# Another order for the gathers of the last read counts, and edge sums one attention step sooner, in a segmented attention kernel

## The chip, the cores and the metric

The kernel runs on one core of a Trainium2 chip. The core has five engines with queues of their own: TensorE (PE, matrix products), VectorE (DVE), ScalarE (ACT), GpSimd (POOL, which here issues all indirect gathers and scatters and does a few elementwise operations) and SyncE (SP, which issues the plain transfers). Sixteen DMA engines are shared by all queues. The metric is the device time of one execution in microseconds. All times in this document are microseconds unless marked otherwise.

## The reference, cut to what matters

```python
N, d = feat.shape                      # 16384, 256;  B = 8, LMAX = 3072
q = feat @ Wq; k = feat @ Wk; v = feat @ Wv          # 32, 32 and 256 columns
starts = jnp.searchsorted(bids, jnp.arange(B))
pos = jnp.arange(N) - starts[bids]
pad = lambda x: jnp.zeros((B, LMAX, x.shape[-1])).at[bids, pos].set(x)
mask = jnp.zeros((B, LMAX), bool).at[bids, pos].set(True)
scores = jnp.where(mask[:, None, :], jnp.einsum('bld,bmd->blm', pad(q), pad(k)), NEG)
rp = jnp.einsum('blm,bmd->bld', jax.nn.softmax(scores, -1), pad(v))
r = rp[bids, pos]
t = r @ Wt
tn = (t - t.mean(0)) / jnp.sqrt(t.var(0) + EPS) * gamma + beta
return feat + jax.nn.relu(tn)
```

The ids in `bids` are not sorted, so `pos` runs far outside a segment's table. A write outside the table is dropped, a negative position counts from the table's end, and of two tokens on one place the later wins. The read `rp[bids, pos]`, though, takes every token: a position outside the table reads the segment's first or last row. Three kinds of rows come out of this: rows that a token owns and that are read once or twice (their "read count"), the sixteen edge rows (first and last row of each segment), which are read by thousands of tokens, and rows of tokens that lost their place and read the winner's row. The mean and the variance over all tokens weigh every row by how often it is read.

## The kernel before

The owned rows of each of the eight segments are listed and gathered from `feat` in up to six tiles of 128 rows. In this data some segments fill four tiles, others more; products of unfilled tiles are skipped by a branch on TensorE. For each segment `e` there are six attention steps `u`, one for each tile of queries (`step`, which calls `attend` and `scale`): TensorE multiplies the exponentials with the values, VectorE takes the reciprocal of the denominators (`rdens`), and ScalarE (even `u`) or VectorE (odd `u`) scales the result into `tk`. After steps 3 and 5 SyncE stores the rows to `t_rows` in memory. Between the steps the next segment is made ready: transposes (`xt_main`, `xt_rest`), projections (`project`), values (`values`) and exponentials (`scores`). For the segment after that, `prefix`, `sizes` and `list_ahead` count the rows, and `list_part` makes the index list and issues the gathers.

The order is written out by hand. A small class records every operation on its engine's queue in the order in which the Python code runs, works out from the memory that it reads and writes which earlier operations it has to wait for, and sets semaphores accordingly. Each engine works through its queue in this order: an instruction that waits holds all behind it. A helper's line stands for all its operations (L803 for products, L878 for gathers, L831 for tensor-scalar operations), so the names of the tiles tell them apart. Short PSUM results are put into two banks in turn by `nb()`: each call takes the other bank, so a product waits until what was in that bank two calls before has been read. On TensorE a predicated (skipped) product's signal is given by the next product that isn't predicated.

Around the change, by line:

- `attend` (L1273) ends with the reciprocal (L1282). It then issues gathers that wait for this reciprocal: in segment 5 (`NB - 3`) one gather of read counts a step (`gather_reads`, L1197), for segment 6; in segment 6 (`NB - 2`) those of segment 7, and the three gathers of winners' rows (`gather_again`, L1201) from `t_rows` into `tl`.
- `rows()` (L1571) returns two lists. Parts of the first run from a work list by `slot()`; its part `e` issues the three gathers `ridl` from `row_of`. `slot(99)` after step 2 of segment 6 (L1815) runs what is left, the last row-wise sums `both` among it. The second list, `late`, is called by number: `late[0]` (`f`, L1606) multiplies the edge rows' numbers over the partitions on TensorE and makes the gather index `eidx` in eight VectorE instructions; `late[1]` (`h`, L1635) makes six one-hot tiles `sel` on GpSimd; `late[2]`, `late[3]` and `late[4]` follow in segment 7 with the weights.
- L1823 to L1825 call `late[0]` and `late[1]` after step 4 of segment 6.
- At the end of segment 6, GpSimd sets `none` to zero (L1856). In segment 7, after step 0, GpSimd gathers the edge rows of the first seven segments into `ecat` (L1751). The sequence of steps is 0, 1, 4, 5, 2, 3; after step 2, TensorE picks the edge rows of segment 7 with `sel`, and VectorE adds them to `ecat` (L1786), ahead of step 3's reciprocal.
- `moments` (L1337) adds rows and their squares, weighted by read counts, into `acc` on VectorE; `square` (L1307) is ScalarE's part. Rows of `tl` come first in segment 7 (L1760).
- After the loop, the products with `ecat` and `acc` (L1872, L1873) give mean and variance; then every group of output rows is put together, stored by SyncE, and the owned rows are scattered over them by GpSimd.
- At the head of a segment (L1790 to L1795) step 0 is followed by `prefix`, `sizes` and `list_ahead` for segment `e + 2`, then by scores, step 1 and `xt_rest`.

```python
            for t in ((), (), (), (0, 1), (2,), ())[u]:
                gather_again(t, paced)
            for t in ((), (0,), (1,), (), (2, 3), (4, 5))[u]:
                gather_reads(e + 1, t, paced)
```

Of the kernel before, what the change touches and what calls it, by code (L numbers as in the profile page):

```python
# [21 lines left out]
NB = 8  # L22
# [8 lines left out]
LT = 3  # L31
# [870 lines left out]
def fast_path(nc, feat, bids, wq, wk, wv, wt, gamma, beta, out, bad):  # L902
# [147 lines left out]
    def nb():  # L1050
        turn[0] += 1
        return ps_m[turn[0] % 2]
# [144 lines left out]
    def gather_reads(e, t, after):  # L1197
        m = e * FT + t
        pg.gather(reads_r[:, m : m + 1], reads_of, idx[:, m : m + 1], N, after=[after])
# [22 lines left out]
    def xt_rest(e):  # L1222
        b = nb()
        for h in range(DH):
            transposes(e, h, range(4, 6), b, h * QB)
        for h in range(DH):
            into_xT(h, QA, QA + QB, b[:, h * QB : (h + 1) * QB])

    def project(e, c, b=None):
        b = nb() if b is None else b  # L1230
        n = QA if c == 0 else QB
        for h in range(DH):
            pg.mm(
                b[:, 0:n], w4[:, h, :], xT[:, h, c * QA : c * QA + n],
                start=(h == 0), stop=(h == DH - 1), pred=over4(e, 4 * c),
            )
        if (e, c) == (0, 1):
            pg.mm(b[:, n : n + 1], ident[:], ones[:, 0:1])
        lo, n = c * QA, (QA if c == 0 else QB)
        qe, ke = q[e % 2], k[e % 2]  # L1240
        pg.act(qe[0:96, lo : lo + n], b[0:96, 0:n], AF.Identity, bias=cqk[0:96, :])
        pg.act(qe[96:P, lo : lo + n], b[0:32, 0:n], AF.Identity, bias=cqk[0:32, :])
        for t in range(n // P):
            g = 32 * t
            pg.copy("DVE", ke[g : g + 32, c, :], b[96:P, t * P : (t + 1) * P])
# [27 lines left out]
    def attend(e, u):  # L1273
        po = po_of[u] = nb() if e == NB - 1 and u in (2, 3) else ps_o[u % 2]
        src, w = (pa, u) if u < 4 else (pb, u - 4)
        for t in (0, 1, 2, 4, 5, 3):
            pg.mm(
                po[:, 0 : D + 1], src[:, t, w * P : (w + 1) * P], vs[e % 2][:, t, :],
                start=(t == 0), stop=(t == 3), pred=over4(e, max(t, u)),
            )  # L1280
        m = e * FT + u
        paced = pg.recip(rdens[:, m : m + 1], po[:, D : D + 1])  # L1282
        if e == NB - 3:
            gather_reads(e + 1, u, paced)
        if e == NB - 2:
            for t in ((), (), (), (0, 1), (2,), ())[u]:
                gather_again(t, paced)
            for t in ((), (0,), (1,), (), (2, 3), (4, 5))[u]:
                gather_reads(e + 1, t, paced)
        if u % 2 and e < NB - 1:  # L1290
            pg.ts(tk[:, m, :], po[:, 0:D], rdens[:, m : m + 1], ALU.mult)

# [390 lines left out]
    def step(e, u, more=None):  # L1683
        attend(e, u)
        if more is not None:
            more()
        scale(e, u)
        if (e, u) != (NB - 1, 1):
            lag.append((e, u))
# [36 lines left out]
    for e in range(NB):  # L1726
        last = e == NB - 1
        n = e + 1
        if e == 1:
            one, two, three_ = edges()  # L1730
            sides = [*side_count(0, below[:]), *side_count(1, above[:])]
            fills = fill_rows()
            work.extend([fills[0], *one, fills[1], two, *sides, fills[2], *three_, lambda: own_of(NB - 1)])
        if not last:
            size_of(n)
        pg.region_of((e,) if last else (e, n))
        if e == 0:
            xt_rest(0)
            values(0, 1)
            project(0, 1)  # L1740
            values(0, 2)
            scores(0, 0, range(4, 6))
            own_of(2)
            zero_fill(2)
        if last:
            for u in (0, 1, 4, 5, 2, 3):
                step(e, u)
                if u == 0:
                    scores(e, 1, range(4))
                    late[2]()  # L1750
                    pg.gather(ecat[:, 0, :], t_rows[0 : (NB - 1) * FW, :], eidx[:], (NB - 1) * FW)  # L1751
                    for g in range(FIRST, EARLY):
                        load_group(g)
                if u == 1:
                    scores(e, 1, range(4, 6))
                    late[4]()
                if u == 4:
                    late[3]()
                if u == 0:
                    lag[:0] = [(NB, t) for t in range(LT)]  # L1760
                if u == 5:
                    first = square(e, 1)
                    for g in range(EARLY, MID):
                        load_group(g)
                if u == 1:
                    pg.act(row_sum[:], ones[:], AF.Identity, scale=reads_r[:, e * FT + 1 : e * FT + 2])
                if u == 3:
                    any_ = hot[0 : 2 * NB, 0:2, :, :].rearrange("p k u x -> p (k u x)")
                    pg.mm(sums[:], none[0 : 2 * NB, :], any_, start=True, stop=False)
                    by_row(row_sum, first[0], first[2])  # L1770
                if u == 3:
                    while lag or squared:
                        if lag and len(squared) < 2:
                            squared.append(square(*lag.pop(0)))
                        else:
                            moments()
                else:
                    past(e)
                if u == 2:
                    b_e = ps_s[0]  # L1780
                    for u_ in (0, 4, 5, 1):
                        pg.mm(
                            b_e[:, 0:D], sel[:, u_, :], tk[:, e * FT + u_, :], start=(u_ == 0), stop=(u_ == 1),
                            pred=over4(e, u_),
                        )
                    pg.tt(ecat[:, 0, :], ecat[:, 0, :], b_e[:, 0:D], ALU.add)  # L1786
                    pg.act(ecat[:, 1, :], ecat[:, 0, :], AF.Square)
        else:
            busy = e + 2 < NB
            step(e, 0, lambda: (xt_main(n, 0), xt_main(n, 1)))  # L1790
            if e + 3 < NB:
                prefix(e + 2, e + 3)
                sizes(e + 2)
            if busy:
                list_ahead(e + 2)  # L1795
            scores(e, 1, range(4))
            past(e)
            slot()
            if e == NB - 2:
                load_group(0)  # L1800
            step(e, 1)
            xt_rest(n)
            project(n, 0)
            if busy:
                list_part(e + 2, 0)
            scores(e, 1, range(4, 6))
            past(e)
            slot(1 if busy else 2)
            step(e, 2, lambda: project(n, 1))
            if busy:  # L1810
                list_part(e + 2, 1)
            past(e)
            slot(1 if busy else 2)
            if e == NB - 2:
                slot(99)  # L1815
                load_group(1)
                load_group(2)
            if e + 3 < NB:
                zero_fill(e + 3)
            step(e, 3)  # L1820
            scores(n, 0, range(4))
            step(e, 4, lambda: values(n, 0))
            if e == NB - 2:  # L1823
                late[0]()
                late[1]()  # L1825
            past(e)
            if e + 4 < NB:
                own_of(e + 3)
            if not busy:
                slot(2)  # L1830
            if e == 3:
                losers()[0]()
            slot()
            step(e, 5)
            values(n, 1)
            past(e)
            if e == 3:
                losers()[1]()
            if e == NB - 4:
                prefix(NB - 1, NB)  # L1840
                sizes(NB - 1)
                pg.copy("DVE", armf[:], arm[:])
                pg.red(cnt_f[0:1, 0:1], armf[:])
                pg.ts(upto[:, NB + 1 : NB + 2], cnt_f[0:1, 0:1], 16.0, ALU.mult, 16.0 * (4 * NB + LT), ALU.add)
                todo, late = rows()
                work.extend(todo)
            scores(n, 0, range(4, 6))
            values(n, 2)
            past(e)
            slot()  # L1850
        if last:
            assert not lag and not squared
        pg.end_region()
        if e == NB - 2:
            slot(99)
            pg.set("POOL", none[:], 0.0)  # L1856
# [104 lines left out]
    for k in range(NG):  # L1961
# [24 lines left out]
        if 3 <= k < 3 + NB:  # L1986
            e = k - 3
# [96 lines left out]
```

## Time and profile before

| | |
|---|---|
| median of three runs | 328.13 (326.43 to 328.25) |
| profiled execution | 328.07 |
| its span, first to last instruction | 323.4 |
| mean granted TensorE clock | 0.874 |
| busy: PE, DVE, ACT, POOL | 252.1, 239.1, 151.0, 136.7 |
| bytes moved | 52.49 MB, mean 162 GB/s |

The stretches that matter here, in us from the span's start: segment 0 begins near 32, segment 6 runs from 193 to 212, segment 7 from 212 to 231, the statistics from 231 to 243, and the output from 243 to the end. How full each stretch is shows the page's second part (forty slices of 8.1 us, tenths of busy time, PEclk the granted clock in tenths, DMA the mean busy share of the sixteen DMA engines):

```profile
PE   5599699998998999899989999696666963632600
...
DVE  3845579989677686559577898963578999999930
...
POOL 7333307061080043304402572688030237887774
PEclk9999979999999999999999999978575798755555
DMA  3101104124055015301210124399596999998895
```

TensorE and VectorE share the load up to slice 27; then the DMA engines and VectorE, and at last GpSimd. One execution is profiled, so a duration in it has no spread of its own.

### The profile page before, as it was taken

The numbers are of one execution on the slowest core, as the hardware profiler recorded it, in microseconds if no ns is written. First come the engines' busy times: TensorE is split into PE (matmuls) and PEld (weight loads), VectorE is DVE, ScalarE is ACT, GpSimd is POOL, SyncE is SP. The second block draws the span as 40 slices with busy tenths as digits, with TensorE's granted clock in tenths as the row PEclk, the third lists the DMA queues.
The fourth block names the chain that finished last, engine by engine and source line by source line (L and its number), as shares of the span: only waits on it lengthen the run. The fifth ranks groups of instructions, "written<-read, shape, count | busy, mean of one in ns | idle before, by whom it ended". The sixth has DMA issues, their size and how long they took to land.

```text
span 323.4 us, 4634 instructions
## 1 busy us (share of the span) xinstructions
PE 252.1 (78%) x1279; PEld 165.0 (51%) x1279; DVE 239.1 (74%) x773; ACT 151.0 (47%) x294; POOL 136.7 (42%) x143
## 2 busy tenths in 40 slices
PE   5599699998998999899989999696666963632600
PEld 2465557665776678667866776474313321210200
DVE  3845579989677686559577898963578999999930
ACT  3136859874765574366547639774301221110000
POOL 7333307061080043304402572688030237887774
PEclk9999979999999999999999999978575798755555
DMA  3101104124055015301210124399596999998895
GB/s 103 32 25 31 36 2 132 47 66 128 3 102 152 0 49 125 101 4 47 76 34 1 51 90 156 144 346 388 181 372 255 375 402 393 421 396 343 313 377 193
DMA packets 21533, 52.49 MB, mean 162 GB/s; under 512 B 5488, under 2 KB 14786, under 8 KB 17530
## 3 DMA queue, kind: packets, MB, share of 16 engines
q1 hardware_dynamic: 15674, 41.37, 34.0%
q0 software_dynamic: 5280, 10.18, 10.8%
q10 hardware_dynamic: 544, 0.52, 0.5%
q8 instruction: 15, 0.25, 0.3%
q14 instruction: 20, 0.16, 0.2%
HBM read 26.27 MB, written 28.74 MB: 170 GB/s over the span
## 4 chain that ended last, share of the span: by engine, by line
PE 47%; DVE 24%; issue 9%; ACT 8%; POOL 7%; DMA 1%; POOLq 1%; DVEq 0%
PE ps L803 45%; DVE tk L822 6%; DVE f L822 5%; POOL out L894 4%; ACT pa L813 3%; PE ps L808 2%; ACT xT L813 2%; DVE junk L829 2%; ACT vs L818 2%; DVE k L819 1%; DMA ecat<-t_rows,eidx 1%; POOL sel L831 1%; DVE tk L1938 1%; DVE tk L1940 1%; POOLq L1072 1%
## 5 line engine op out<-in xcount | busy, mean ns | idle before, releaser
L878 POOL DMA_INDIRECT xs<-in_r_feat,idx x48 | 50.9, 1061 | 100.5 <-DVE idx L842 51.9
L803 PE MATMUL ps<-vs,pa 128*128 128x257 f32 x312 | 77.9, 395 | 4.1 <-ACT vs L818 3.8
L803 PEld LDWEIGHTS ps<-vs,pa 128*128 128x128 f32 x312 | 58.3, 194 | 17.4 <-ACT vs L818 5.9
L894 POOL DMA_INDIRECT out<-tk,idx x32 | 35.9, 1121 | 31.8 <-DVE tk L842 17.6
L803 PE MATMUL ps<-wvt,xT 128*128 128x256 f32 x156 | 38.0, 390 | 3.4 <-ACT vs L818 3.4
L803 PE MATMUL ps<-y,hot 32*128 32x256 bf16 x256 | 14.9, 366 | 28.5 <-DVE f L822 25.6
L818 ACT COPY f<-ps 128x1024 f32<-128x1024 f32 (+1 forms) x12 | 10.0, 834 | 57.7 <-PE ps L803 57.7
L803 PEld LDWEIGHTS ps<-wvt,xT 128*128 128x128 f32 x156 | 29.0, 191 | 13.5 <-ACT vs L818 4.6
L813 ACT ACTIVATE pa<-ps,mask 128x512 f32<-128x512 f32 x48 | 29.5, 686 | 12.1 <-PE ps L803 12.1
L803 PEld LDWEIGHTS ps<-y,hot 32*128 32x128 bf16 x256 | 6.8, 115 | 44.9 <-DVE f L822 36.5
L803 PE MATMUL ps<-f,ident 128*128 128x512 f32 x38 | 27.4, 845 | 1.3 <-DVE f L822 1.2
L822 DVE TENSOR_TENSOR f<-f,ps 128x1024 f32<-128x1024 f32 (+3 forms) x17 | 25.9, 1559 | 0.9 <-PE ps L803 0.9
L842 DVE SCALAR_TENSOR_TENSOR acc<-tk,reads_r,acc 128x256 f32<-128x256 f32 x45 | 21.5, 477 | 5.7 <-DMA reads_r<-reads_of,idx 4.2
L819 DVE COPY k<-ps 32x128 f32<-32x128 f32 x48 | 14.1, 294 | 15.6 <-PE ps L803 14.9
L813 ACT ACTIVATE xT<-ps,negx 128x512 f32<-128x512 f32 (+1 forms) x32 | 17.0, 582 | 17.3 <-PE ps L808 9.8
L818 ACT COPY vs<-ps 128x512 f32<-128x512 f32 x24 | 14.1, 589 | 20.9 <-PE ps L803 20.8
L813 ACT ACTIVATE q<-ps,cqk 96x512 f32<-96x512 f32 (+3 forms) x32 | 18.3, 573 | 10.4 <-PE ps L803 10.1
L855 DVE RECIPROCAL rdens<-ps 128x1 f32<-128x1 f32 x48 | 7.7, 160 | 19.6 <-PE ps L803 19.5
L803 PE MATMUL ps<-xT,w 128*128 128x512 f32 (+1 forms) x48 | 21.8, 581 | 0.0
L878 POOL DMA_INDIRECT reads_r<-reads_of,idx x12 | 13.2, 1098 | 19.9 <-DVE ge L831 11.7
L842 DVE SCALAR_TENSOR_TENSOR acc<-sq,reads_r,acc 128x256 f32<-128x256 f32 x45 | 21.5, 478 | 0.0
L813 ACT ACTIVATE pb<-ps,mask 128x256 f32<-128x256 f32 x48 | 19.2, 476 | 4.1 <-PE ps L803 3.8
(271 smaller groups left out, 433.0 us busy)
## 6 DMA issues: line engine op xcount, KB each, us to landing
f<-in_r_feat SPq DMA_DIRECT2D x16, 1024.0 KB, 8.1
out<-f SPq DMA_DIRECT2D x15, 1024.0 KB, 8.5
t_rows<-tk SPq DMA_DIRECT2D x8, 512.0 KB, 3.5
t_rows<-tk SPq DMA_DIRECT2D x8, 256.0 KB, 2.9
eb<-edge_of SPq DMA_DIRECT2D x16, 64.0 KB
out<-f SPq DMA_DIRECT2D x2, 512.0 KB, 2.7
xs<-in_r_feat,idx POOLq DMA_INDIRECT x48, 2.9
out<-tk,idx POOLq DMA_INDIRECT x39
```

What stands on the lines that cost most here:

```text
L803: "PE", lambda e: e.matmul(out, lhsT, rhs, start=start, stop=stop, skip_group_check=True),
L808: return self.op("PE", lambda e: e.transpose(out, in_, ident), [in_, ident], [out], pred=pred)
L813: "ACT", lambda e: e.activation(out, in_, func, bias=bias, scale=scale), [in_, *more], [out]
L818: return self.op("ACT", lambda e: e.copy(out, in_), [in_], [out])
L819: return self.op(eng, lambda e: e.tensor_copy(out, in_), [in_], [out])
L822: return self.op(eng, lambda e: e.tensor_tensor(out, a, b, op), [a, b], [out])
L829: lambda e: e.tensor_scalar(out, a, s1, s2, op0, op1, accum_out=accum)
L831: else e.tensor_scalar(out, a, s1, s2, op0, op1),
L842: else e.scalar_tensor_tensor(out, a, s, b, op0, op1),
L855: return self.op("DVE", lambda e: e.reciprocal(out, in_), [in_], [out])
L878: lambda e: e.indirect_dma_start(out=out, out_offset=None, in_=table, in_offset=bass.IndirectOffsetOnAxis(ap=ind, axis=0), bounds_check=n ...
L894: lambda e: e.indirect_dma_start(out=table, out_offset=bass.IndirectOffsetOnAxis(ap=ind, axis=0), in_=src, in_offset=None, bounds_check=n ...
```

## The change

Three orders change; no operation is added or removed.

1. In segment 6, `attend` issues the gathers of read counts for segment 7 two a step in steps 0 to 2, and all three gathers of winners' rows in step 3. Before, the read counts were spread over steps 1, 2, 4 and 5, and the winners' rows over steps 3 and 4.
2. `late[0]` and `late[1]`, the edge product with its index and the one-hot rows, are called before step 4 of segment 6 instead of after it. Since step 4 issues no gathers any more, and step 5 neither, all gathers of this segment stand ahead of the one-hots on GpSimd.
3. In segment 0 alone, `prefix`, `sizes` and `list_ahead` for segment 2 are called after step 1 and `xt_rest` instead of after step 0. The values passed to them are the same.

```diff
         if e == NB - 2:
-            for t in ((), (), (), (0, 1), (2,), ())[u]:
+            for t in range(2 * u, 2 * u + 2) if u < 3 else ():
+                gather_reads(e + 1, t, paced)
+            for t in range(LT) if u == 3 else ():
                 gather_again(t, paced)
-            for t in ((), (0,), (1,), (), (2, 3), (4, 5))[u]:
-                gather_reads(e + 1, t, paced)
...
             step(e, 0, lambda: (xt_main(n, 0), xt_main(n, 1)))
-            if e + 3 < NB:
+            if 0 < e < NB - 3:
                 prefix(e + 2, e + 3)
                 sizes(e + 2)
-            if busy:
+            if 0 < e and busy:
                 list_ahead(e + 2)
             scores(e, 1, range(4))
...
             step(e, 1)
             xt_rest(n)
+            if e == 0:
+                prefix(e + 2, e + 3)
+                sizes(e + 2)
+                list_ahead(e + 2)
             project(n, 0)
...
             scores(n, 0, range(4))
-            step(e, 4, lambda: values(n, 0))
             if e == NB - 2:
                 late[0]()
                 late[1]()
+            step(e, 4, lambda: values(n, 0))
             past(e)
```

On the queues this gives, for GpSimd in segment 6:

```
before: ridl x3, reads 0, reads 1, tl x3, reads 2, reads 3, sel x6, reads 4, reads 5, none, ecat
after:  reads 0, reads 1, ridl x3, reads 2, reads 3, reads 4, reads 5, tl x3, sel x6, none, ecat
```

On TensorE the edge product stands ahead of the values of segment 7 instead of behind their first pair, so the two banks of `nb()` swap their turns there; in segment 0 the two products of `prefix` stand behind step 1, with the same swap. SyncE's order doesn't change.

## The prediction

> **What bounds the kernel now.** I read the shares of the chain of waits first, then that chain in order of time between 186 and 242 us, then GpSimd's and VectorE's timelines there, because the change acts there. The chain over the whole span:
>
> ```profile
> PE 47%; DVE 24%; issue 9%; ACT 8%; POOL 7%; DMA 1%; POOLq 1%; DVEq 0%
> ```
>
> TensorE carries most of the span, so most of the span is out of this change's reach. But the seven per cent of POOL lie in one place, ahead of the statistics (start us, us, what):
>
> ```profile
> 217.12 0.71 POOL sel L831
> ...
> 217.93 1.91 POOL sel L831
> ...
> 224.80 4.58 DMA ecat<-t_rows,eidx
> ...
> 229.40 0.43 DVE ecat L822
> ...
> 229.85 0.42 ACT ecat L813
> 230.27 0.37 ACT tk L813
> ...
> 230.69 5.24 PE ps L803 x6
> ```
>
> The one-hot rows (sel) keep GpSimd busy, the gather of the edge rows (ecat) is issued after them, its landing releases VectorE's sum, and ScalarE's scaling and TensorE's last products follow. GpSimd's own timeline tells why that gather is so late; in brackets stand the idle time before an instruction and what ended it:
>
> ```profile
> 193.18 0.99 POOL L878 DMA_INDIRECT reads_r<-reads_of,idx  x1 [1.12 <-DVE tk L831]
> 199.50 0.99 POOL L878 DMA_INDIRECT ridl<-row_of,idxo  x1 [5.33 <-DVE tk L831]
> ...
> 203.47 1.75 POOL L878 DMA_INDIRECT reads_r<-reads_of,idx  x1 [0.30 <-issue]
> 206.56 1.25 POOL L878 DMA_INDIRECT reads_r<-reads_of,idx  x1 [1.35 <-DVE k L819]
> 208.51 0.99 POOL L878 DMA_INDIRECT tl<-t_rows,ridl  x1 [0.70 <-DVE zrow L842]
> ...
> 214.98 6.75 POOL L831 TENSOR_SCALAR sel<-edge,rcol 128x128 f32<-128x128 f32 x6
> 222.01 1.09 POOL L878 DMA_INDIRECT reads_r<-reads_of,idx  x1 [0.27 <-issue]
> 223.41 1.01 POOL L878 DMA_INDIRECT reads_r<-reads_of,idx  x1 [0.30 <-issue]
> 224.41 0.22 POOL L861 MEMSET none<- 128x128 bf16 x1
> 224.80 1.01 POOL L878 DMA_INDIRECT ecat<-t_rows,eidx  x1 [0.17 <-issue]
> ```
>
> From 208.51 on it never rests; before that it rests three times. VectorE behind it stands still twice:
>
> ```profile
> 226.80 0.48 DVE L842 SCALAR_TENSOR_TENSOR acc<-tk,reads_r,acc 128x256 f32<-128x256 f32 x1 [4.20 <-DMA reads_r<-reads_of,idx]
> ...
> 229.40 0.42 DVE L822 TENSOR_TENSOR ecat<-ecat,ps 128x256 f32<-128x256 f32 x1 [1.72 <-DMA ecat<-t_rows,eidx]
> ```
>
> Of these the second counts: without the first wait VectorE would merely reach the second sooner.
>
> [...] for the one-hots: they take from 0.71 to 1.91 us, and the longest lies at 217.93 under four 0.47 us accumulations of VectorE. [...] TensorE idled 2.39 us up to 39.12 and the granted clock was 0.50 from 41 to 43 us.
>
> **The change, part by part.**
>
> *1. GpSimd's order in segment 6.* The stretch from 199.50 to 224.80 us (25.30 us) holds twelve gathers (three ridl, six reads, three tl), six one-hots and a memset. The changed stream holds the same, all gathers first, so no work is removed: all that can be won is idle time and blocking.
> - Start. The first gather now waits for the reciprocal of step 0 (VectorE, 197.66 to 197.82). From such a release to the gather it took 0.76, 0.83 and 0.85 us (206.56, 199.50, 208.51), so it starts at 198.6 instead of 199.50: 0.9 us won.
> - Rests. The two reads of step 0, the three ridl and the two reads of step 1 run back to back at a pitch of 1.30 us to about 207.5; the release of step 2 (205.80) and of step 3 (207.66) are past by then. The rests of 1.35 and 0.70 shrink to the 0.30 of plain issue: 1.05 + 0.40 = 1.45 us.
> - Blocking. Two reads took 1.75 and 1.25 instead of 1.0 beside VectorE's work; another gather may meet it now. Won 0 to 1.0; I take 0.25.
> - One-hots. Six take 6.75 us; at the shortest, 0.71 each, it would be 4.3. Part 2 brings four accumulations (215.26 to 216.96) forward, out of their time. Won 0 to 2.4; I take 0.5.
>
> Sum 0.9 + 1.45 + 0.25 + 0.5 = 3.1 us: the ecat gather at 221.7 instead of 224.80. Its landing took 4.58. The DMA queue is fuller there (409 to 434 GB/s between 220 and 223 against 272 to 401 from 224 to 227): a reads gather issued at 222.01 released VectorE at 226.80, 4.8 us; the tl gathers took 5.6 to 6.9, the ridl ones 2.3. I take 4.7, losing 0.1, with bounds of 2.3 either way.
>
> *What is queued behind.* The tl gathers go from 208.51, 209.81 and 211.15 to about 210.3, 211.6 and 213.0, and with 6.4 us of landing are there at 216.7, 218.0 and 219.4. ScalarE squares them at 217.04 (two) and 219.01, ahead of the scaling of steps 1 and 4 of the last segment in its queue; it loses about 1 us. VectorE's sums of these rows follow. Both must be done at about 226.4, when the gather lands, and before they had idled 1.2 (ScalarE at 221.78) and 1.12 + 4.20 us there, the latter two on reads that have now landed long ago: no cost. Without that cover each us of lateness would cost one.
>
> *2. Edge sums one step sooner (late[0] and late[1] ahead of step 4).* One product of 0.39 us now stands before the values of the next segment and waits for VectorE's reduction ending at 205.60: TensorE, free at 204.6, loses 1.0 us. In return the two PSUM banks swap turns: the second pair of values, which waited 2.72 us for ScalarE's copy until 209.59, now waits for VectorE's last read of the edge product, 208.8. VectorE's chain of eight small instructions moves ahead of one reciprocal; ScalarE's scaling waits 0.2 us longer, beside its own backlog. [...] at 0.50 eight products of the last segment took 3.12 instead of 1.98 us. TensorE may so come 0.7 to 2.2 us sooner into the last segment. I count that at nothing by itself: the cover is the ecat gather, for which TensorE idles from 228.2 to 230.7 anyhow. One remainder: the six last products ran 5.24 us at clock 0.50; if the clock falls later they gain 0 to 1.0. I take 0.25.
>
> *3. Segment 0: prefix, sizes and list_ahead of segment 2 after xt_rest.* Thirteen VectorE instructions and two tiny products move behind step 1. The product waited for a PSUM bank and held attention behind it:
>
> ```profile
> 39.12 0.18 PE L803 MATMUL ps<-lm,tri 128*128 128x1 bf16 x1 [2.39 <-ACT xT L813]
> ...
> 42.13 2.65 PE L803 MATMUL ps<-xT,w 128*128 128x512 f32 x4
> ```
>
> Attention step 1 now starts at 36.8. But the banks swap here too: the projection (42.13) now needs the bank that ScalarE's next pair of xT copies reads, and these stand behind four exponentials (to 41.69) and take 0.84: 42.55. There TensorE has idled 2.6 us; at full clock the projection takes 1.88 (as at 60.28), at the halved one 2.65. VectorE, idle for 1.76 us until 44.83, waits for its end at 44.45 to 45.2, then runs without a rest to 58. So −0.35 to +0.9 us, passed on whole; I take 0.3 lost. The moved VectorE work fits into its idle time.
>
> *4. Behind the statistics.* From 243.49 VectorE, and from 265.89 GpSimd (a put every 1.29 us up to 318.81), work without a rest longer than 1.1 us; the DMA engines are full from 251 on, but with transfers that start after the statistics. So what is won at 229.40 is won at the end.
>
> Sum: 3.1 − 0.1 + 0.25 − 0.3 = 2.95 us. The profiled execution took 328.07 (span 323.4 and 4.67 around it), 0.06 under the median of the three runs: 328.07 − 2.95 = **325.1 us**.
>
> **The rivals.** One per cent is 3.28 us, about what a measurement of this kernel can tell from no change; the line lies at 324.85.
> - *The larger gain.* The one-hots run nearly free (4.8 us, 2.0 won instead of 0.5) and the gather lands in 3.9. For it: five 1 MB loads that now crowd the queue from 206 to 222 may go sooner with part 2. Against: VectorE's sums still have to be made. 325.1 − 1.5 − 0.8 = 322.8.
> - *It doesn't do what it says.* GpSimd's work ahead of the gather is unchanged; blocking and one-hots win nothing, the gather lands in 5.5, segment 0 loses 0.9: 328.07 − 2.35 + 0.9 + 0.9 = 327.5.
> - *Slower: the tl rows become the wait.* Behind three 1 MB loads (about 7.9 us at 400 GB/s) plus two more and their stores they could land far later. From the third row's landing L it is a square, two sums, two reciprocals and two more pairs of sums to the edge sum, about 2.8 us, so it decides from L = 223.6 and is slower than before from 226.6, 13.6 us after issue. At L = 230 it gives 328.07 + 3.4 + 0.3 = 331.8. Against: no gather here took over 7.6.
>
> **The numbers.** Forecast 0.72 (own range 323.6 to 326.6), larger gain 0.13, nothing done 0.10, slower 0.05. The forecast's 0.72 falls about half on each side of 324.85. Faster 0.36 + 0.13 = 0.49; within one per cent 0.36 + 0.10 = 0.46; slower 0.05. Range 322.8 to 327.6: it takes in the two middle rivals' times; the bounds of single terms don't add up in one run.
>
> **What would show it.** Step 1: the first reads gather near 198.6, no rest of GpSimd over 0.4 us up to the one-hots, which start at 214 to 215; ecat follows them at once near 221.7 and VectorE's wait on reads (4.20) is gone. Step 2: no 2.72 us wait of TensorE at 209.6. Step 3: attention at 36.8, VectorE's key copies between 44.5 and 45.3. Wrong, if VectorE waits for tl rows or squares when ecat has landed, if the gather lands over 6 us after issue, or if segment 1 starts over 1 us later.

## The result and the profile after

Before, the median was 328.13 (326.43 to 328.25); after, 323.9 (323.04 to 325.25). The ratio of the runs is 0.9887 with an interval of 0.9837 to 0.9936: 1.1% faster, 3.7 us, with 2.1 and 5.3 as the interval's ends. The profiled execution after took 323.04, its span is 318.4. A ratio compares only the runs within 1.5% of the fastest of their kernel (further down 2 of 4 for parts 1 and 2 at first, 3 of 5 with the ecat gather ahead of the one-hots, 4 of 20 with the tl gathers late, 11 of 23 for before beside the single parts), so the medians of all runs are given with it.

Executions of one kernel differ: 27 runs of before on one chip lay between 321.87 and 329.32. Much of that arises ahead of segment 0, as the second row of the table shows (the kernel before, profiled again). So stages are compared from the first reciprocal of segment 6 on. Times are those at which VectorE, GpSimd or TensorE starts the work named, read from the timelines; "again" is a second profile of the same kernel, and the last four rows are experiments further down.

| kernel | first attention product | key copies, segment 1 | first reciprocal, segment 6 | ecat gather issued | ecat sum | last products done | first output sum | last put |
|---|---|---|---|---|---|---|---|---|
| before | 33.88 | 44.83 | 197.66 | 224.80 | 229.40 | 235.96 | 243.49 | 318.81 |
| before, again | 30.00 | 39.26 | 192.08 | 219.57 | 223.66 | 230.21 | 237.82 | 313.13 |
| after | 32.68 | 44.27 | 197.27 | 219.79 | 226.66 | 231.91 | 239.15 | 313.10 |
| after, again | 34.21 | 44.51 | 197.33 | 219.60 | 225.75 | 231.03 | 238.27 | 312.22 |
| part 1 alone | 33.90 | 44.85 | 197.84 | 220.27 | 227.03 | 231.16 | 238.49 | 313.77 |
| parts 1 and 2 | 34.16 | 45.12 | 198.11 | 220.35 | 227.19 | 233.65 | 241.29 | 316.56 |
| parts 1 and 2, again | 33.06 | 44.00 | 196.81 | 219.55 | 225.38 | 229.51 | 236.88 | 310.84 |
| the same, third load held | 32.98 | 43.92 | 196.75 | 219.87 | 222.90 | 228.00 | 235.38 | 313.19 |

From the first reciprocal of segment 6 to the last put it is 121.15 and 121.05 before, 115.83 and 114.89 after: 5.2 to 6.3 us less. Both profiles of before agree to 0.1 us here, while their ends lie 5.7 us apart, which is why this stretch carries the argument. It has a spread too, though: the two profiles of parts 1 and 2 take 118.45 and 114.03. Of these 4.4 us, 2.3 lie in the last products, 1.6 behind them and 1.0 in the gather's landing, with 0.5 the other way in its issue. What is steady is the issue of the ecat gather: 27.1 and 27.5 us after the first reciprocal of segment 6 in the two profiles of before, 22.2 to 23.1 in the six below them, all of kernels with part 1.

The chain of waits over the span, after:

```profile
PE 41%; DVE 26%; ACT 11%; issue 9%; POOL 6%; DMA 4%; another core or an unknown queue 1%; POOLq 1%; DVEq 0%; SPq 0%
```

and the same chain in order of time at the end of segment 7 (start us, us, what):

```profile
219.42 0.20 POOL none L861
...
219.79 6.85 DMA ecat<-t_rows,eidx
226.64 0.02 issue
226.66 0.43 DVE ecat L822
...
227.12 0.42 ACT ecat L813
227.54 0.37 ACT tk L813
227.91 0.04 issue
227.95 3.94 PE ps L803 x6
```

The path still runs over the ecat gather. It is issued 5.0 us sooner (4.6 counted from the first reciprocal of segment 6), but its landing takes 6.9 us instead of 4.6, and the six products take 3.9 instead of 5.2. GpSimd's timeline after (in brackets the idle time before an instruction and what ended it):

```profile
198.19 0.99 POOL L878 DMA_INDIRECT reads_r<-reads_of,idx  x1 [4.40 <-DVE rdens L855]
...
203.39 1.47 POOL L878 DMA_INDIRECT ridl<-row_of,idxo  x1 [0.30 <-issue]
205.17 1.00 POOL L878 DMA_INDIRECT reads_r<-reads_of,idx  x1 [0.30 <-issue]
...
212.98 1.00 POOL L878 DMA_INDIRECT tl<-t_rows,ridl  x1 [0.31 <-issue]
214.08 5.29 POOL L831 TENSOR_SCALAR sel<-edge,rcol 128x128 f32<-128x128 f32 x6
219.42 0.20 POOL L861 MEMSET none<- 128x128 bf16 x1
219.79 1.09 POOL L878 DMA_INDIRECT ecat<-t_rows,eidx  x1 [0.16 <-issue]
```

No rest is over 0.31 us, and the one-hots take 5.29 instead of 6.75. VectorE's timeline after:

```profile
215.72 0.17 DVE L855 RECIPROCAL rdens<-ps 128x1 f32<-128x1 f32 x1 [3.55 <-PE ps L803]
...
226.66 0.42 DVE L822 TENSOR_TENSOR ecat<-ecat,ps 128x256 f32<-128x256 f32 x1 [1.95 <-DMA ecat<-t_rows,eidx]
```

Its wait for read counts has gone; the one for ecat has stayed, 1.95 instead of 1.72. The wait at the head of segment 7 is 3.55 us instead of 2.44 (at 215.04 before). ScalarE's timeline shows where it comes from ("remote" is a release that the profile can't name):

```profile
213.90 0.58 ACT L818 COPY vs<-ps 128x512 f32<-128x512 f32 x1 [3.88 <-remote]
```

This copy reads TensorE's second values of segment 7, and TensorE had gone on to the attention behind them at 210.35.

### The profile page after: what moved, and what is told of

Read it like the earlier page. It is cut to its first block, busy times and chain, and to the rows that moved or that the text cites. A ratio compares the mean times of both kernels' runs of the same rounds, so it can differ in the third digit from the quotient of the medians.

```text
span 318.4 us, 4632 instructions
## 1 busy us (share of the span) xinstructions
PE 249.3 (78%) x1279; PEld 162.2 (51%) x1279; DVE 238.8 (75%) x773; ACT 150.3 (47%) x294; POOL 133.8 (42%) x143
## 4 chain that ended last, share of the span: by engine, by line
PE 41%; DVE 26%; ACT 11%; issue 9%; POOL 6%; DMA 4%; another core or an unknown queue 1%; POOLq 1%; DVEq 0%; SPq 0%
PE ps L803 39%; DVE tk L822 6%; DVE f L822 5%; POOL out L894 4%; ACT pa L813 4%; ACT xT L813 2%; PE ps L808 2%; DMA ecat<-t_rows,eidx 2%; ACT vs L818 2%; DMA t_rows<-tk 2%; DVE junk L829 2%; DVE k L819 1%; DVE tk L1942 1%; DVE tk L1944 1%; ACT xs L818 1%
## 5 line engine op out<-in xcount | busy, mean ns | idle before, releaser
L894 POOL DMA_INDIRECT out<-tk,idx x32 | 34.4, 1075 | 28.4 <-DVE tk L842 19.2
L803 PE MATMUL ps<-f,ident 128*128 128x512 f32 x38 | 29.0, 893 | 1.7 <-DVE f L822 1.2
L813 ACT ACTIVATE q<-ps,cqk 96x512 f32<-96x512 f32 (+3 forms) x32 | 18.4, 573 | 13.6 <-PE ps L803 13.2
L878 POOL DMA_INDIRECT reads_r<-reads_of,idx x12 | 12.0, 1003 | 23.0 <-DVE ge L831 11.7
```

The source lines that it names most:

```text
L803: "PE", lambda e: e.matmul(out, lhsT, rhs, start=start, stop=stop, skip_group_check=True),
L813: "ACT", lambda e: e.activation(out, in_, func, bias=bias, scale=scale), [in_, *more], [out]
L878: lambda e: e.indirect_dma_start(out=out, out_offset=None, in_=table, in_offset=bass.IndirectOffsetOnAxis(ap=ind, axis=0), bounds_check=n ...
L894: lambda e: e.indirect_dma_start(out=table, out_offset=bass.IndirectOffsetOnAxis(ap=ind, axis=0), in_=src, in_offset=None, bounds_check=n ...
```

## The experiments

### The three parts, one by one

Part 1, the gathers' order, is the first hunk of the diff alone:

```diff
-            for t in ((), (), (), (0, 1), (2,), ())[u]:
+            for t in range(2 * u, 2 * u + 2) if u < 3 else ():
+                gather_reads(e + 1, t, paced)
+            for t in range(LT) if u == 3 else ():
                 gather_again(t, paced)
-            for t in ((), (0,), (1,), (), (2, 3), (4, 5))[u]:
-                gather_reads(e + 1, t, paced)
```

> Part 1 of the change alone: two read-count gathers a step in steps 0 to 2 and the three tl gathers in step 3 of segment 6, on the kernel before; the edge product stays behind step 4 and segment 0 as it was. GpSimd's order is then already that of the changed kernel. Theory A (filled rests of GpSimd bring the gain): GpSimd without a rest from about 198.6 us on, ecat gather issued at 220 to 222 instead of 224.80, time 323.5 to 325.5. Rival B (the product and the swap of PSUM banks in part 2 bring it): within 0.5 us of before, 327.6 to 328.6. Rival C (the order in segment 0 brings it): the same as B. Also looked at: TensorE's 2.72 us wait at 209.6 should stay, since the banks don't swap.

Measured: 323.07, just below theory A's range, ratio 0.9837 (0.9790 to 0.9884). The ecat gather went out at 220.27 and its sum came at 227.03, 29.19 after the first reciprocal of segment 6 instead of 31.74. Part 1 alone gains as much as the whole change: its ratio is no worse than the whole change's 0.9887, and its last put comes 115.93 after that reciprocal, against 115.83 and 114.89. That parts 2 and 3 add anything to it is not shown.

Part 2, the edge product one step sooner, is the last hunk alone (`late[0]` and `late[1]` ahead of step 4).

> Part 2 alone: late[0] and late[1] before step 4, gathers of segment 6 in the old steps, so that GpSimd makes the one-hots between the second and the third tl gather and issues tl 2 and reads 2 to 5 behind them. Theory A: GpSimd's rests at 199.5 and 206.6 stay and the ecat gather is issued at 224 to 225 as before; third tl row and the reads land after 221, and VectorE waits for them; 327 to 329.5. Rival B: TensorE's shorter wait at 209.6 gives 324 to 326 by itself.

Measured: 325.74 (320.7 to 326.42), in rival B's range, but too uneven for a ratio; before had 327.95 beside it. SyncE's timeline has the three loads of segment 7:

```profile
211.75 1.97 SPq L1722 DMA_DIRECT2D f<-in_r_feat  x3
```

and VectorE's the ecat sum, without a wait ahead of it:

```profile
228.02 0.41 DVE L822 TENSOR_TENSOR ecat<-ecat,ps 128x256 f32<-128x256 f32 x1
```

The loads start at 211.75 instead of 213.12, as TensorE gets there sooner. The gather goes out at 223.91, only 0.9 us sooner than before, yet VectorE doesn't wait for it: it landed within 4.1 us, and the sum is 30.16 after the first reciprocal, 1.6 better. In this profile, then, part 2 is worth something without part 1; the times do not settle it.

Part 3, segment 0, is the middle hunks alone.

> Part 3 alone: prefix, sizes and list_ahead of segment 2 after step 1 and xt_rest in segment 0. Theory A: no gain, from attention step 0 to the first key copy 11.3 to 11.9 us instead of 11.0, and 328.0 to 329.0 in all. Rival C: 324 to 326.

Measured: 328.5, ratio 1.0048 (1.0018 to 1.0078). The medians of all runs, 328.5 and 327.95, lie only 0.55 us apart, so the loss of 1.6 us that the ratio gives is not shown. In the profile, segment 0 loses nothing: from the first attention product to the key copies it takes 10.39 instead of 10.95. VectorE waits longer for the ecat gather, issued at 223.45:

```profile
230.12 0.42 DVE L822 TENSOR_TENSOR ecat<-ecat,ps 128x256 f32<-128x256 f32 x1 [3.88 <-DMA ecat<-t_rows,eidx]
```

It landed after 6.65 us. SyncE's timeline tells more. It has a fourth load in this segment, which stands ahead of the gather here:

```profile
222.37 0.33 SPq L1722 DMA_DIRECT2D f<-in_r_feat  x1
```

That is 1.1 us ahead of the gather. Part 2 alone issues this load behind its gather (227.58). What that means for the landing is taken up where the prediction is discussed.

Parts 1 and 2 together, without part 3:

> Parts 1 and 2, without part 3 (segment 0 as before). Theory A: as the changed kernel or up to 0.9 us faster, 323.0 to 324.5, since part 3 was priced at 0.3 us lost (-0.35 to +0.9). Rival C (segment 0 brings the gain): 326 to 328. From attention step 0 of segment 0 to the first key copy of list_part (11.0 us before, 11.6 in the changed kernel's profile) it should be 11.0 again.

Measured: 322.73 (317.26 to 326.1), ratio 0.9740 (0.9652 to 0.9829), four uneven runs; it is repeated below. Its profile, of the execution of 326.1, is the row "parts 1 and 2" of the table.

### What the landing of the ecat gather depends on

All three loads of segment 7 held until the gather has landed, in the changed kernel (the first waits, the others are behind it on SyncE):

```diff
-                    pg.gather(ecat[:, 0, :], t_rows[0 : (NB - 1) * FW, :], eidx[:], (NB - 1) * FW)
+                    edges_in = pg.gather(ecat[:, 0, :], t_rows[0 : (NB - 1) * FW, :], eidx[:], (NB - 1) * FW)
...
-                        load_group(g)
+                        load_group(g, [edges_in] if g == FIRST else ())
```

> After with one wait added: the first of the three loads of feat that SyncE issues in segment 7 (at 215.47 in after) waits until the ecat gather has landed, and the two loads and the stores behind it on SyncE with it. Theory A, the gather's 6.87 us of landing are queueing behind these loads: with the load of segment 6 long drained, the gather lands 2.3 to 4.0 us after its issue, near 222.5 to 224, VectorE's ecat sum comes before the last reciprocal has to wait for it, and the end of segment 7 is bound by its own attention instead: last products at 226 to 227.5. The loads are late by 7 to 8 us, which may hold the output at 244 to 250; time 321 to 325. Theory B, the gather's landing is a fixed latency plus its own descriptors: it still takes 6 to 7 us, the loads are later for nothing, time 324 to 328. ScalarE's 3.9 us stall at 210 to 213.9 comes before these loads: unchanged under both.

Measured: 327.08, beside 328.37 for before, ratio 0.9982 (0.9952 to 1.0012). GpSimd's timeline has the gather's issue:

```profile
220.55 1.10 POOL L878 DMA_INDIRECT ecat<-t_rows,eidx  x1 [0.16 <-issue]
```

and SyncE's the loads that wait for its landing:

```profile
223.50 1.43 SPq L1722 DMA_DIRECT2D f<-in_r_feat  x3
```

The loads were released at 223.50, so the gather had landed in 2.95 us: theory A on the landing, though not on the time, which it put at 321 to 325. The sum came 29.2 us after the first reciprocal of segment 6, hardly sooner than in the changed kernel (29.4): VectorE no longer waits for the gather, but TensorE's attention of segment 7 is late here (first reciprocal at 218.42). And the loads are paid for: from the first output sum to the last put it took 79.20 us, against 73.95 and 75.32 after and before.

The gather moved ahead of the one-hots, behind step 5 of segment 6:

```diff
             step(e, 5)
+            if e == NB - 2:
+                pg.gather(ecat[:, 0, :], t_rows[0 : (NB - 1) * FW, :], eidx[:], (NB - 1) * FW)
+                late[1]()
             values(n, 1)
```

> After with the ecat gather moved from segment 7 to the end of segment 6, ahead of the one-hot rows, and the one-hots with it. Theory A, the chain gather order - one-hots - ecat landing is what still sets the end: the gather is issued when the last store of rows has landed, near 215, at most 217, lands by 222, the wait of VectorE for it (1.95 us in after) is gone, and the last six products start 1 to 2 us sooner, near 226 to 227; the time is 1 to 2.5 us less than after's 323.9, 321.5 to 323. Theory B, segment 7's attention, late by ScalarE's stall, sets the end just as well: the wait for the gather goes but the sum becomes late for the one-hots' product, ScalarE or step 3; time within 0.7 us of after. The one-hots, now behind the gather on GpSimd, end near 221 to 223; over 225 they would be the new wait, and the time then over 325.

Measured: 326.86, beside 328.37 for before; ratio 0.9883 (0.9825 to 0.9941). GpSimd's timeline:

```profile
220.17 1.00 POOL L878 DMA_INDIRECT ecat<-t_rows,eidx  x1 [3.85 <-DMA t_rows<-tk]
221.26 7.15 POOL L831 TENSOR_SCALAR sel<-edge,rcol 128x128 f32<-128x128 f32 x6
```

It waits for the store of segment 6's rows, 3 us past the latest time expected, and the one-hots, now behind it, end at 228.4, late enough to be the new wait that the expectation names. VectorE's wait for the gather is gone, yet its sum comes 29.1 us after the first reciprocal of segment 6, hardly sooner than in the changed kernel (29.4): theory B in that.

The two loads of segment 6 moved to segment 7, so that none is in flight from 205 to 212:

```diff
-                load_group(1)
-                load_group(2)
...
-                    for g in range(FIRST, EARLY):
+                    for g in range(1, EARLY):
```

> After with the two loads of feat of segment 6 (issued at 205.43) moved to segment 7, in front of the other three: no load is in flight between 205 and 213. Theory A, ScalarE's stall (3.88 us in front of its copy at 213.90, released by nothing that it waits for) [...]: the copy runs within 1 us of the end of TensorE's values, near 210.5 to 211.5, VectorE's first reciprocal of segment 7 comes at 212 to 213.5 instead of 215.72. Theory B, the stall comes from GpSimd's gathers being denser: it stays at 3 to 5 us. The price under both: five loads after 212 crowd the queue until about 226, so the ecat gather lands later (7 to 9 us), and the time is between 322 and 327.

Measured: 324.55, beside 328.37 for before; ratio 0.9892 (0.9860 to 0.9925). ScalarE's timeline:

```profile
215.83 0.58 ACT L818 COPY vs<-ps 128x512 f32<-128x512 f32 x1 [4.52 <-remote]
```

The stall stays without the loads of segment 6, so theory A falls for these; the five loads begin at 212.15, 0.8 us into the wait. The gather, now behind five loads, was in 7.6 us after its issue.

### Controls, and a mechanism of the slower rival

In parts 1 and 2, the tl gathers behind the one-hots:

```diff
-            for t in range(LT) if u == 3 else ():
-                gather_again(t, paced)
+            if u == 3:
+                paced_of["tl"] = paced
...
                 late[1]()
+                for t in range(LT):
+                    gather_again(t, paced_of["tl"])
```

> Parts 1 and 2 of the change without part 3, and the three gathers of winners' rows (tl) issued behind the one-hot rows instead of ahead of them: GpSimd issues no gather between the last read counts (about 209 to 210) and the one-hots' end (about 216), the tl gathers run at 216 to 220 and the ecat gather after them near 220.5. Two questions. The late rows: the prediction's slower rival put 2.8 us from the landing of the third tl row to the edge sum, deciding from a landing at 223.6. With 5.6 to 6.9 us of landing the third row is there at 225 to 226.5, so VectorE's ecat sum should come at 228 to 229.3 instead of 227.2, 1 to 2 us of loss: 324 to 326 where parts 1 and 2 had a median of 322.7. If the rows don't matter, time as parts 1 and 2. The stall: theory A, TensorE's signal for the second values of segment 7 (and with it ScalarE's copy) is late because GpSimd issues gathers back to back just then: with the one-hots there instead, the copy runs at 211 to 212 with under 1 us of wait. Theory B, it has to do with something else that the change moves: the wait of 4 to 5 us stays.

> The changed kernel itself, beside parts 1 and 2 alone on the same chip, to see what part 3 is worth in their company. From part 3 alone (ratio 1.0048, 1.6 us) theory A says 1 to 2 us slower than parts 1 and 2 alone. Theory B, part 3 costs only its 0.3 to 0.6 us in segment 0 and the rest of 1.6 us was the ecat gather's landing behind other loads: within 0.7 us of parts 1 and 2. Its ratio to before should again be near 0.9887; its profile should again show ScalarE's copy of the second values waiting 3 to 5 us for TensorE's signal near 214, if that belongs to the order and not to one execution.

> Parts 1 and 2 without part 3 once more, with five rounds: as the version that may beat the changed kernel. Theory A: 321.5 to 323, a ratio to before of 0.980 to 0.985. Theory B: the lone run of 317.3 of the first look was an outlier of that chip and it stands where after stands, 0.986 to 0.989.

> The kernel before, profiled in the same way as the experiments, as a control for three waits read from one execution each. If ScalarE's late copy belongs to GpSimd's new order, its second copy of values near 212 waits under 1 us here, as in the first profile of before, while the smaller late signals of TensorE near 75 and 94 us, which part 2 and part 3 alone show too, may appear. The ecat gather should again be issued at 224 to 225, and land 4.6 to 6.7 us later, depending on whether the fourth load of segment 7 (222.85) is in front of it.

Measured on one chip: the tl gathers late, 326.32 and ratio 0.9918 (0.9865 to 0.9972); the changed kernel, 321.56 and 0.9899 (0.9826 to 0.9972); parts 1 and 2, 320.74 and 0.9867 (0.9799 to 0.9934), a ratio that is theory B's; before, 326.54. The profiled execution of before took 322.61; its ecat gather landed in 4.1 us, less than expected, and its second copy of values waited 1.99 us (1.91 in the first profile). The intervals of the second and third ratio overlap, so what part 3 costs in company is not settled. ScalarE's timeline with the tl gathers late:

```profile
222.27 0.42 ACT L813 ACTIVATE sq<-tl 128x256 f32<-128x256 f32 x1 [6.36 <-DMA tl<-t_rows,ridl]
```

and TensorE's:

```profile
224.48 2.07 PE L803 MATMUL ps<-tk,sel 128*128 128x256 f32 x4 [7.24 <-ACT pb L813]
```

The first tl row landed at 222.25, instead of 215.6 in parts 1 and 2. ScalarE stands before its square, the scaling and exponentials behind it wait, and TensorE with them for 7.24 us. The third row came at 224.2, and the edge sum at 227.53: 3.3 us behind, where the rival had put 2.8. In time, the ratios put the loss against parts 1 and 2 at 0.0051, 1.7 us, with overlapping intervals; by the medians of all runs it is 5.6 us, nearly the whole gain, and in the profiles the stretch to the last put is 120.30 instead of 114.03. The wait is shown, its size is not settled.

The second profile of the changed kernel, ScalarE's timeline:

```profile
210.62 0.59 ACT L818 COPY vs<-ps 128x512 f32<-128x512 f32 x1 [0.53 <-PE ps L803]
```

and VectorE's:

```profile
216.79 0.50 DVE L842 SCALAR_TENSOR_TENSOR acc<-tl,ones,acc 128x256 f32<-128x256 f32 x1 [1.79 <-DMA tl<-t_rows,ridl]
...
225.75 0.42 DVE L822 TENSOR_TENSOR ecat<-ecat,ps 128x256 f32<-128x256 f32 x1 [2.64 <-DMA ecat<-t_rows,eidx]
```

The 3.88 us stall is not there: the same kernel has it in one execution and not in another, so the order alone does not bring it. It cost little, too: the reciprocal at the head of segment 7 is 3.3 us sooner without it (212.43), the ecat sum 0.9. And in the kernel before itself the one-hots took 7.11 us in the second profile, 6.75 in the first:

```profile
209.40 7.11 POOL L831 TENSOR_SCALAR sel<-edge,rcol 128x128 f32<-128x128 f32 x6
```

### A version that may beat both

Parts 1 and 2, and only the third load held: as in the first diff of the part before, with `g == EARLY - 1` in place of `g == FIRST`.

> Parts 1 and 2 without part 3, and only the third of the three loads of feat in segment 7 held until the ecat gather has landed. In the look at parts 1 and 2 the gather went out at 219.55 and landed at 225.35, 5.8 us, with three loads of 1 MB queued from 211.7 on; with all three held it landed 2.9 us after its issue, but the output took some 4 us more. Theory A, the gather lands when what was queued ahead of it has gone, and one load of 1 MB is 2.6 us at the 400 GB/s seen there: it lands 2.5 to 4 us after issue, near 222.5 to 223.5, VectorE's 3.0 us wait for it goes, the last products start 1.5 to 2.5 us sooner; and one late load of three is made up for, as the output is bound by GpSimd's puts: ratio 0.980 to 0.984, median 318.5 to 320. Theory B, the late load is given back in the output as with three: ratio 0.985 to 0.990, the wait gone all the same. Theory C, the load held isn't what the gather queues behind: it still takes over 5 us.

Measured: 321.11, ratio 0.9836 (0.9801 to 0.9871). The windows view (stretch, length; busy time and instructions of PE, PEld, DVE, ACT and POOL; granted clock, DMA share, GB/s) of parts 1 and 2:

```profile
220.00:222.00 2.00, 2.00 (x6) 1.63 (x5) 2.00 (x8) 1.97 (x7) 0.65 (x1) 0.50 1.00 418
222.00:224.00 2.00, 2.00 (x7) 1.12 (x6) 0.36 (x1) 0.99 (x3) 0.00 (x0) 0.67 1.05 363
```

and with the third load held:

```profile
220.00:222.00 2.00, 2.00 (x6) 1.55 (x5) 2.00 (x8) 1.97 (x7) 1.18 (x1) 0.50 0.21 64
222.00:224.00 2.00, 2.00 (x7) 1.24 (x6) 1.15 (x4) 1.57 (x5) 0.00 (x0) 0.71 0.12 39
```

With two loads ahead the queue is nearly empty from 220 on (64 and 39 GB/s instead of 418 and 363), and the gather lands in 3.0 us instead of 5.8. The ecat sum is 2.5 us sooner, the first output sum 1.5, and then 3.9 us are lost to the last put (77.81 against 73.96): theory B's mechanism, though the ratio lies in theory A's range. The likely reason is the 3.3 us in which the DMA engines idled (2 us at a share of 0.21, 2 us at 0.12). That the output can hardly make them up is an estimate: in the changed kernel the share was 0.95 to 1.02 from 255 to 290, and 0.75 to 0.78 from there to 300. The chain with the third load held shows what would be next:

```profile
211.16 6.68 DMA tl<-t_rows,ridl
217.84 0.02 issue
217.87 0.42 ACT sq L813
218.28 0.36 ACT tk L813
218.65 0.37 ACT pb L813
219.02 0.04 issue
219.07 8.91 PE ps L803 x25
```

VectorE's wait for ecat is down to 0.52 us and off the chain: a tl row releases ScalarE's square, and that holds TensorE. It is faster than before; whether it beats parts 1 and 2 or the changed kernel the overlapping intervals do not tell (0.9836 against 0.9867 and 0.9899).

## Why the prediction was right

The forecast, 325.1, was 1.2 us above the measured median, and the larger gain's 322.8 was 1.1 below it. The mechanism was the right one: GpSimd's order brings the ecat gather forward, and the end with it. But four terms were off and partly cancelled, so the closeness of the sum is in part luck. From the first reciprocal of segment 6 to the last put, first profile of each kernel:

| term | forecast, won | measured, won | from |
|---|---|---|---|
| ecat gather issued | 3.1 | 4.62 | 27.14 and 22.52 after the reciprocal |
| its landing | −0.1 | −2.27 | issue to sum, 4.60 and 6.87 |
| last products | 0.25 | 1.31 | sum to products done, 6.56 and 5.25 |
| behind | 0 | 1.66 | products done to last put, 82.85 and 81.19 |
| sum | 3.25 | 5.32 | |

The first two terms, which are the forecast's mechanism, won 2.35 instead of 3.0. The last two won 2.97 instead of 0.25. That is luck as far as the runs show: each of them varies by about as much between two profiles of one kernel, as shown below.

*Where the path lies.* The seven per cent of POOL do not lie in one place. The page lists the chain by line:

```profile
PE ps L803 45%; DVE tk L822 6%; DVE f L822 5%; POOL out L894 4%; ACT pa L813 3%; PE ps L808 2%; ACT xT L813 2%; DVE junk L829 2%; ACT vs L818 2%; DVE k L819 1%; DMA ecat<-t_rows,eidx 1%; POOL sel L831 1%; DVE tk L1938 1%; DVE tk L1940 1%; POOLq L1072 1%
```

Four of the seven are puts of the output (L894), and the one-hots are one. Nor is TensorE's 47% most of the span. The chain in order of time, on which the forecast rests, was read rightly.

*Gathers' order.* Start (0.92 won) and rests (none over 0.31) came as predicted. The one-hots won 1.46 instead of 0.5, and what is left over, 0.79, stands against the 0.25 taken for blocking: the twelve gathers took 13.31 us before and 12.45 after. Both lie inside the bounds that were given. The one-hots' gain can't be put down to the order alone: they took 5.29 and 5.05 after, 6.75 and 7.11 before, but 5.41 with part 3 alone. The first reads gather (198.19), the one-hots' start (214.08) and the missing waits are the signs that were named.

*The landing is the step that failed.* One of the prediction's signs against itself, a landing over 6 us, came up in both profiles. I took 4.7 for 4.58, reasoning from throughput at the moment of issue, and named only bounds of 2.3 either way; the upper one was needed. In the runs the landing goes with what is queued ahead of the gather: 6.87 us with three loads of 1 MB issued in the 4.3 us before it, 2.95 with the three held back. SyncE's timeline has, before:

```profile
213.12 1.43 SPq L1722 DMA_DIRECT2D f<-in_r_feat  x3
...
222.85 0.33 SPq L1722 DMA_DIRECT2D f<-in_r_feat  x1
```

and after:

```profile
215.47 1.43 SPq L1722 DMA_DIRECT2D f<-in_r_feat  x3
```

The three loads start with TensorE's progress into segment 7, not with GpSimd's: before, SyncE waits 1.5 us for a product of TensorE ahead of them. A gather issued sooner therefore stands nearer behind them. The fourth load matters too, where it stands ahead of the gather (us):

| profile | gather issued after the first of the three loads | gather issued after the fourth load | landing |
|---|---|---|---|
| before | 11.7 | 2.0 | 4.6 |
| before, again | 12.0 | 3.3 | 4.1 |
| after | 4.3 | load is behind | 6.9 |
| after, again | 8.3 | load is behind | 6.1 |
| part 2 alone | 12.2 | load is behind | 4.1 at most |
| part 3 alone | 11.5 | 1.1 | 6.65 |

With one of the three loads held back the landing was 3.0, with five ahead 7.6.

The packets in the traces agree: the last packet of SyncE's transfers in that stretch starts 6.0 us after the gather's issue with part 3 alone, 3.9 and 3.3 in the two profiles of before, 1.6 with part 2 alone, and the gather's own last packet ends 0.3 us after it (0.8 with part 2 alone).

The landing and SyncE's last packet go together there; what ties the one to the other the traces don't show. Of what was won at the issue, half was given back here in the first profile, a third in the second (4.87 won, 1.55 lost).

*Part 2, costed at nothing.* TensorE did come sooner, where the stall didn't hold it: in the second profile segment 7's first reciprocal comes 15.1 us after segment 6's instead of 17.4, in the first 18.4. No 2.72 us wait is left in either. What that is worth in the whole change is not settled, as part 1 alone measures no slower.

*Clock.* The products took 3.94 at a clock of 0.85, then 0.50, instead of 5.24: 1.3 won, more than the bound of 1.0. This is no merit of the order. In parts 1 and 2, the same products took in the first profile

```profile
228.48 5.15 PE ps L803 x6
```

and in the second, at a granted clock of 1.00 throughout,

```profile
226.66 2.82 PE ps L803 x6
```

So 2.3 us of the path came or went between two executions of one and the same program. In the first, two pairs of the products took 2.07 and 2.08 us, as at the clock of 0.50 in before; in the second, 1.12 each. What makes them differ the profiles don't show.

*Part 3.* The first profile took 11.59 from first attention product to key copies, 0.64 more than before, as the granted clock was 0.50 from 42 to 45 and the projection took 3.20; the second took 10.30, 0.65 less, with 1.98 for the projection (1.88 at a clock of 1.00 in segment 1 of before). That is wider than the forecast's −0.35 to 0.9: six profiles with part 3 took 10.30 to 12.20, seven without it 10.94 to 10.96, and an eighth, before again, 9.26. The idle time of TensorE ahead of the projection was 2.35 us in both profiles of after; the projection behind it took 3.20 in the first and 1.98 in the second. The term of 0.3 is neither confirmed nor refuted.

*Behind the statistics.* The shift was passed on, and 1.4 us more from the first output sum to the last put (73.95 against 75.32), which I had not foreseen. The change need not be its cause: parts 1 and 2 took 75.27 in the first profile and 73.96 in the second, part 1 alone 75.28, part 2 alone 74.02. What decides between the two values is open.

*Rivals.* The larger gain was the nearer one for the one-hots, and wrong on the landing. Nothing waited for tl rows when ecat had landed; with these gathers moved 5.6 us later the rival's wait appeared.

## What to carry to other kernels

A small gather's landing is no constant: the same one took 2.95 to 7.6 us here. Date it from the bulk loads queued ahead of it, the last one above all (3.0 us with the third alone held back), and ask which engine starts those. Issuing it sooner, into a fuller queue, can give back part of the gain (2.27 of 4.62 us here); in the two runs that emptied the queue for it, the loads held back were paid for with 3.9 to 5.3 us in the output. A forecast that comes out right should be checked term by term, and a term that differs between two profiles of one kernel is nobody's gain. And before explaining a new stall, profile the same kernel again.

## What had not been expected of the hardware

- ScalarE's copy of TensorE's second values can run several us after the last product that it reads: the copy at 213.90 waited 3.88 us, that at 215.83 waited 4.52, and the profile names no release. SyncE's three loads have the same in after: they wait 4.3 us for an unnamed release, where they wait 1.5 us for TensorE before. That a signal of TensorE is seen late is thus possible, not shown.
- That wait of ScalarE was there, at 3.1 to 5.5 us, in six profiles of kernels with part 1, and absent in the second profiles of after and of parts 1 and 2, with the tl gathers late, and with the third load held. The loads of segment 6 are not its cause, and the gathers' order alone is not. The chip may matter: of the nine profiles with part 1 whose chip is known, the five on two chips have it and the four on two others don't. So may the recording: the six profiles with the wait hold 203 to 207 updates of TensorE's semaphores, the four without it 226 to 228, so an unnamed release may be one that was not recorded. The cause is open.
- The landing goes with that wait: the three loads start at 215.5 to 216.3 with it and at 211.3 to 211.8 without, and the ecat gather behind them took 6.7 to 6.9 us with it (part 1 alone, parts 1 and 2, after), 5.5 to 6.1 without (tl gathers late, parts 1 and 2 again, after again).
- The ecat gather took 2.95 to 3.0 us behind a nearly empty queue, and 5.5 to 7.6 us behind three to five loads of 1 MB issued within the 8.4 us before it.
- Six one-hot tiles on GpSimd took from 4.8 to 7.2 us in kernels that differ only in order.
